# A transformer block in Strassen form: another order of the MLP's buffers, the last sum of y behind attention's sums, and an operand's sums later

## The chip, the cores and the metric

The kernel runs on one core of one Trainium2 chip. The metric is the time of one execution on the device, in microseconds. The kernel before took 735.64 us, the median of 3 runs (734.81 to 736.56).

## What is computed

One cross-attention block with its MLP, all in float32. `x` and `ctx_2048` are both 8 x 256 x 512. The block's batch is 8, its queries come from `x`, its keys and values from `ctx_2048`; there are 16 heads of 32.

```python
x = layer_norm(hidden_states, ln1_w, ln1_b)
q = (x @ q_w + q_b)                      # 512 -> 512, then 16 heads of 32
k = (encoder_hidden_states @ k_w + k_b)
v = (encoder_hidden_states @ v_w + v_b)
attn = softmax(mask(q @ k.T / sqrt(32)))
out = (attn @ v) @ cproj_w + cproj_b
hidden = out + residual                  # residual: hidden_states
y = layer_norm(hidden, ln2_w, ln2_b)
y = gelu(y @ fc_w + fc_b)                # 512 -> 2048, tanh form
return hidden + y @ proj_w + proj_b      # 2048 -> 512
```

## The kernel before

**Groups and stages.** The 8 batch rows are taken two at a time: four groups, g = 0 to 3, of 512 tokens. A first stage makes attention for all four groups; a second stage, the MLP, then runs over the four groups again. Between the stages the hidden state of each group lies in DRAM (`hid_dram`), and `load_hid` brings it back.

**Strassen products.** Each large matrix product is a 2 x 2 block product in Winograd's form of Strassen: seven block products in place of eight, and sums of blocks before and after. An operand is a tile of seven slots: the quarters 11, 12, 21, 22 and three sums. `A_SUMS` are the four sums of a weight operand, `B_SUMS` those of a token operand (the last is t4 = 21 - t2, written after attention's tokens have been turned into columns). `sum_up` makes them one by one. The first MLP product (512 -> 2048) uses the form twice, one inside the other: seven outer products, k = 0 to 6 (`product`), each of seven inner ones (`sub`). So its weight is seven operands of seven slots, each 1792 KB. They are made once, during attention, kept in `w2_dram`, and loaded again for each group by `load_w2`, into four places that are reused in turn. Each call of `product` ends with the load into the place that it has just read; SP issues that load when the product's last matmul is done.

**Attention's order.** The work is written out by hand. A unit is a pair of batch row and 128 columns of heads (8 units in a group). For a unit the kernel turns the probabilities of unit n (`turn_probs`), divides those of unit n + 1 on POOL (`divide`), makes the scores of unit n + 2, and calls what is listed for places in the unit: `between[g, u, i]` holds pieces with matmuls (the projections of the next group, the output projections of earlier ones), `aside[g, u, i]` holds sums, loads and stores; aside 0 runs ahead of the division, 1 to 3 behind it, in this order. `begin` and `spread` fill these lists. `split("b", (i, g, u, at), ...)` lists sum i of the weight operand b (outer operand s3) at such places, all on POOL. Each engine, and SP's queue of DMA issues, works in the order in which the calls are made.

**The end of attention.** After the last unit comes the output projection of group 3 (`project_out(3)`, tiles po). Its second inner product reads the sums of the attention tile, which `sum_att(3, NHG - 1, V)` makes on DVE (tile as, line 735). Group 0's y, the MLP's first input, has its four sums on DVE listed in units 6 and 7 of group 3 (line 993; tile y, line 219), and `split_y` makes the sums of the inner form between the pieces of po (line 307). `project_out` adds the bank to a tile of the residual (resx, 2 KiB per partition, one for each quarter: res11, res12, res21, res22) on POOL (line 630) and stores it to `hid_dram` (line 631).

**The MLP.** In an outer product, the first bank is copied to u1 (ACT, line 1276), u2 = bank 6 + u1 and u3 = bank 7 + u2 follow on DVE (line 1121, a helper that records all such adds). Bank 7 is then accumulated further by TensorE, after u3 has read it. The results go to the hidden quarters h11, h12, h21, h22 or, through a working tile s3 (`hs` in the trace), by POOL adds to several of them. Product 0 writes h21 alone, product 1 h11, product 3 h12, product 4 h22. Between the products the gelus of finished quarters run on ACT. Then seven products with the second weight follow (tiles pw, banks py). The residual comes back into resm (`residual`, line 290) and receives the result.

**Buffers.** A pool gives its tiles addresses in the order of their first call. The MLP's pools lie over those of attention; a tile waits for whatever last used its memory, a DMA's read of it included. In KiB of a partition, near the top:

| attention | at | MLP before | at |
|---|---|---|---|
| pr (probabilities, 3) | 176.4 to 200.4 | h21 | 181.9 to 189.9 |
| v (2) | 200.4 to 204.4 | h22 | 189.9 to 197.9 |
| pt (turned probabilities, 4) | 204.4 to 212.4 | s3 | 197.9 to 205.9 |
| res11 | 212.4 to 214.4 | u1 | 205.9 to 207.9 |
| res12 | 214.4 to 216.4 | u2 (2) | 207.9 to 211.9 |
| res21 | 216.4 to 218.4 | u3 | 211.9 to 213.9 |
| res22 | 218.4 to 220.4 | resm | 213.9 to 221.9 |

Of the kernel before, what the change touches and what calls it, by code (L numbers as in the profile page):

```python
# [10 lines left out]
F32 = mybir.dt.float32  # L11
# [5 lines left out]
P = 128  # L17
# [5 lines left out]
def tile_xattn_block(  # L23
# [62 lines left out]
    HI, HC, HF, HD2 = INNER // 2, NC // 2, NF // 2, D // 2  # L86
# [57 lines left out]
    def place(name, at):  # L144

        return Operand(wts.tile([P, 7, HC, S], F32, tag=f"w{at}", name=name))
# [23 lines left out]
    def rows_of(t):  # L170
        return t.rearrange("p i h s -> p i (h s)")
# [16 lines left out]
    def load_w2(at):  # L188
# [20 lines left out]
    B_SUMS = (  # L209
        ("t1", "12", "11", ALU.subtract),  # L210
        ("t2", "22", "t1", ALU.subtract),
        ("12", "22", "12", ALU.subtract),
        ("t4", "21", "t2", ALU.subtract),
    )

    def sum_up(eng, x, table, *which):
        for i in which:
            to, a, b, op = table[i]
            eng.tensor_tensor(x[to], x[a], x[b], op)
# [73 lines left out]
    ys, hids, y2s = {}, {}, {}  # L293
# [29 lines left out]
    with ExitStack() as att:  # L323
        work = att.enter_context(tc.tile_pool(name="attwork", bufs=2))
# [289 lines left out]
        def load_res(g, *which):  # L614
            for n in which:
                r = work.tile([P, 2, S], F32, tag=f"res{n}", bufs=1, name=f"resx_{g}_{n}")
                nc.sync.dma_start(r, quarter_of(group_of(xf, g), n))
                res[g, n] = r
# [108 lines left out]
        def sum_att(g, hg, eng=nc.gpsimd):  # L727

            x, h = att_in[g], hg % HC
            for to, a, b in (  # L730
                (("t1", "12", "11"),)
                if hg < HC
                else (("t2", "22", "t1"), ("12", "22", "12"), ("t4", "21", "t2"))
            ):
                eng.tensor_tensor(x[to][:, h, :], x[a][:, h, :], x[b][:, h, :], ALU.subtract)
# [10 lines left out]
        def begin(g, u, i, f, *args):  # L746
            aside[g, u, i].append(lambda: f(*args))

        def spread(g, places, pieces):

            for i, f in enumerate(pieces):
                begin(g, *places[min(i, len(places) - 1)], f)
# [31 lines left out]
        V, GP = nc.vector, nc.gpsimd  # L784
# [6 lines left out]
        ALL = (0, 1, 2, 3)  # L791
# [129 lines left out]
        def split(key, *places):  # L921

            for i, *at in places:
                begin(*at, lambda i=i: sum_up(GP, fc[key], A_SUMS, i))
# [3 lines left out]
        sums("b", "a", "b", ALU.subtract, (0, 2, 1), (0, 2, 1), (0, 2, 2), (0, 2, 2))  # L928
        split("a", (0, 0, 3, 1), (1, 0, 3, 2), (2, 0, 3, 2), (3, 0, 4, 1))
        begin(0, 4, 2, keep_own, "a", "11")  # L930
        split("b", (0, 0, 4, 2), (1, 0, 5, 1), (3, 0, 5, 2))
        begin(0, 4, 3, fc_load, "a", "22")

        sums("a", "a", "b", ALU.subtract, (0, 6, 2), (0, 6, 2), (0, 6, 1), (0, 7, 1))
# [25 lines left out]
        g = 1  # L960
        begin(g, 6, 1, load_res, 0, *QUARTERS)
        begin(g, 7, 1, bias_res, 0)
        g = 2
# [6 lines left out]
        g = NG - 1  # L970
# [19 lines left out]
        for c, (u, i) in enumerate(((5, 1), (5, 1), (6, 1), (6, 1))):  # L990
            between[g, u, i].append(lambda c=c: th(c))

        spread(g, [(6, 2), (7, 1), (7, 2), (7, 2)], [lambda i=i: sum_up(V, ys[0], B_SUMS, i) for i in ALL])

        def run(pieces):
            for p in pieces:
# [89 lines left out]
        o = project_out(3)  # L1086
        load_res(3, "12")
        sum_att(3, NHG - 1, V)
        y2 = rows_of(place("y2_0", "v").t).rearrange("p i s -> p (i s)")[:, : 21 * P]
        y2 = y2.rearrange("p (t n s) -> p t n s", t=3, n=7)  # L1090
        for i in ALL:
# [8 lines left out]
    with ExitStack() as mlp:  # L1100
        wpool = mlp.enter_context(tc.tile_pool(name="mlpw", bufs=1, reuse_waits="tile"))
        work = mlp.enter_context(tc.tile_pool(name="mlpwork", bufs=1, reuse_waits="tile"))
# [7 lines left out]
        V, GP = nc.vector, nc.gpsimd  # L1110
# [6 lines left out]
        def mm(ps, lhsT, rhs, first, last):  # L1117
            nc.tensor.matmul(ps, lhsT, rhs, start=first, stop=last, skip_group_check=True)  # L1118

        def add(eng, to, a, b, op=ALU.add):  # L1120
            eng.tensor_tensor(to, a, b, op)  # L1121
# [4 lines left out]
        def load_pw(*which):  # L1126
            for n in which:
                f, d = (int(n[0]) - 1) * HF, (int(n[1]) - 1) * HD2
                nc.sync.dma_start(
                    pw[n], proj_w.rearrange("(c p) n -> p c n", p=P)[:, f : f + HF, d : d + HD2]  # L1130
                )
# [23 lines left out]
        for g in range(NG):  # L1155

            h = {
                n: work.tile([P, 2, HF, P], F32, tag=f"h{n}", name=f"h{n}_{g}")
                for n in ("11", "12", "21", "22", "s3")
            }  # L1160

            def out_quarter(b, k):
# [3 lines left out]
            def us(n, name):  # L1166
                return work.tile([P, 2, S], F32, tag=f"u{n}", bufs=2 if n == 2 else 1, name=f"{name}_{g}")

            def bank_of(n, name):
                return ps_f.tile(  # L1170
                    [P, 2, S], F32, tag=f"f{n}", bufs=2 if n in (1, 5) else 1, name=f"{name}_{g}"
                )
# [18 lines left out]
            def norm_piece():  # L1191

                if g + 1 < NG:
                    if not norm:
                        norm.append(layer_norm(hids[g + 1], f"m{g + 1}", nc.scalar))
                        seen, roots, _ = norm[0]
                        norm.extend([*seen, *roots])
                    norm.pop(1)()
# [14 lines left out]
            def some_gelus(n=3):  # L1213
                for f in gelus[:n]:
                    f()
                del gelus[:n]
# [13 lines left out]
            def block(n, cd):  # L1230
                c, d = int(cd[0]) - 1, int(cd[1]) - 1
                return h[n][:, d, c * HF // 2 : (c + 1) * HF // 2, :]

            def product(k, *sums):


                wt, yn = w2[g, k], QI[FC_ORDER[k][1]]
                bank = {}

                def y_of(n):  # L1240
                    if n in QUARTERS:
                        return ys[g].t[:, yn, int(n[0]) - 1, ts(int(n[1]) - 1, P)]
                    return y2s[g][:, ("t1", "t2", "t4").index(n), yn, :]

                def sub(n, w, b, first, last):
                    if first:
                        bank[n] = bank_of(n, f"pf{n}_{k}").rearrange("p i (j s) -> p (i j) s", j=2)
                    for m in range(HF // 2):
                        mm(
                            bank[n][:, m, :],  # L1250
                            wt[:, QI[w], ts(m, P)],
                            y_of(b),
                            first and m == 0,
                            last,
                        )

                def u(n):
                    return us(n, f"u{n}_{k}").rearrange("p i (j s) -> p (i j) s", j=2)

                def made(cd, n, x):  # L1260
                    some_gelus()
                    if k in (3, 4) and cd != "22":
                        norm_piece()
                    if sums[0][1] is None:
                        add(V, block(sums[0][0], cd), bank[n], x)
                        return

                    r = h["s3"][:, parts[0] % 4 // 2, parts[0] % 2 * HF // 2 :][:, : HF // 2]
                    parts[0] += 1
                    add(V, r, bank[n], x)  # L1270
                    for to, base in sums:
                        add(GP, block(to, cd), block(base, cd), r)

                sub(1, "11", "11", True, False)
                u1 = u(1)
                nc.scalar.copy(u1, bank[1])  # L1276
                sub(6, "s2", "t2", True, True)
                u2 = u(2)
                add(V, u2, bank[6], u1)
                some_gelus()  # L1280
                sub(7, "s3", "12", True, False)
                u3 = u(3)
                add(V, u3, bank[7], u2)
                some_gelus()
                sub(5, "21", "t1", True, False)
                made("22", 5, u3)
                sub(1, "12", "21", False, True)
                some_gelus()
                for to, base in sums:
                    if base:  # L1290
                        add(V, block(to, "11"), bank[1], block(base, "11"))
                    else:
                        nc.scalar.copy(block(to, "11"), bank[1])
                sub(7, "22", "t4", False, True)
                made("21", 7, u2)
                sub(5, "s4", "22", False, True)
                made("12", 5, u2)
                load_w2(w2_place[g, k])
# [8 lines left out]
            product(3, ("12", "21"))  # L1307
            if g == 0:
                load_pw("11", "12", "22")
            product(4, ("22", "12"), ("21", "21"))  # L1310
            if g == 0:
                load_pw("21")
# [139 lines left out]
```

## Time and profile before

| | |
|---|---|
| median of 3 runs | 735.64 us (734.81 to 736.56) |
| the profiled execution | 735.38 us |
| its span | 733.5 us |
| granted TensorE clock, mean over the span | 0.995 |
| TensorE (PE) busy | 722.2 us, 98% of the span |
| POOL, DVE, ACT busy | 502.4, 415.4, 322.3 us |
| moved by DMA | 138.83 MB, mean 189 GB/s |

The profile is of one execution. PE is TensorE's matmuls, PEld its weight loads, DVE VectorE, ACT ScalarE, POOL GpSimd, SP the engine that issues the DMAs here; L1121 is line 1121 of the kernel. A float32 matmul stands twice in the counts: 28 matmuls of an outer product are 56 records. In the strips of slices the span is cut into 40 equal parts of 18.3 us; a digit is the busy share in tenths, and PEclk the granted clock in tenths of full speed. The waits name an engine and line, what ended the wait, the total, the number and the longest. The chain is followed back from the last instruction to what released each step.

### The profile page before, as it was taken

Reading aid. Unit: us, or ns where it says so; the run is one execution under the profiler, and the core shown is the slowest. Engines: PE = TensorE matmul, PEld = TensorE weight load, DVE = VectorE, ACT = ScalarE, POOL = GpSimd, SP = SyncE. Lnnn points to the kernel's source line nnn. Section 1 sums busy time; section 2 is a strip of 40 time slices with the busy share of each in tenths; the row PEclk is TensorE's granted clock in tenths of the full one; section 3 lists DMA queues with packets and bytes.
Section 4 is the critical chain, followed back from the end, with each engine's and each line's share of the span. In section 5 each row is a group of like instructions: output and inputs, shape, how many; then the busy total and the mean of one; then the engine's idle time right before and its main releaser. Section 6 shows DMA issues by size and latency. Waiting matters only on the chain.

```text
span 733.5 us, 14067 instructions
## 1 busy us (share of the span) xinstructions
PE 722.2 (98%) x5109; PEld 630.2 (86%) x5109; DVE 415.4 (57%) x1056; ACT 322.3 (44%) x904; POOL 502.4 (68%) x451
## 2 busy tenths in 40 slices
PE   9999999999999999999799999999999999999998
PEld 7888777887778777778699889998899988999986
DVE  4576756675456566878378585780156811566211
ACT  2277798777676788761034400225002160030500
POOL 3857798987797999886269960589404896048870
PEclk9999999999999999999899999999999999999999
DMA  9516555697639777832699802992019930172001
GB/s 304 186 60 200 207 190 200 200 321 259 221 129 310 251 259 256 295 98 87 229 382 347 347 1 70 390 322 96 0 58 352 338 130 0 58 265 95 1 0 58
DMA packets 75380, 138.83 MB, mean 189 GB/s; under 512 B 6916, under 2 KB 45104, under 8 KB 72624
## 3 DMA queue, kind: packets, MB, share of 16 engines
q1 hardware_dynamic: 75056, 137.91, 53.8%
q8 instruction: 41, 0.67, 0.4%
q14 instruction: 27, 0.22, 0.1%
q0 software_dynamic: 256, 0.02, 0.0%
HBM read 104.36 MB, written 33.55 MB: 188 GB/s over the span
## 4 chain that ended last, share of the span: by engine, by line
PE 91%; POOL 3%; issue 2%; DMA 2%; ACT 2%; DVE 0%; SPq 0%; POOLq 0%; DVEq 0%
PE py L1118 25%; PE pf L1118 23%; PE ppt L699 8%; PE pv L441 7%; PE pqT L441 7%; PE pkT L441 5%; PE s L646 5%; PE av L715 4%; PE po L441 4%; PE pkT L538 2%; POOL resx L630 1%; ACT h L1220 1%; DMA hid_dram<-resx 1%; PE pxt L274 1%; PE pyt L274 1%
## 5 line engine op out<-in xcount | busy, mean ns | idle before, releaser
L1121 POOL TENSOR_TENSOR h<-h,hs 128x512 f32<-128x512 f32 x100 | 126.8, 1291 | 127.0 <-DVE hs L1121 126.4
L1118 PE MATMUL pf<-y,w 128*128 128x128 f32 x1568 | 177.9, 277 | 5.3 <-DVE u L1121 5.3
L1118 PEld LDWEIGHTS pf<-y,w 128*128 128x128 f32 x1568 | 177.7, 194 | 5.7 <-DVE u L1121 5.5
L688 POOL TENSOR_TENSOR pr<-pr,rsum 128x512 f32<-128x512 f32 x128 | 129.5, 1041 | 36.8 <-DVE rsum L686 23.9
L674 ACT ACTIVATE pr<-pr,nmax 128x256 f32<-128x256 f32 x256 | 127.9, 504 | 35.4 <-DVE nmax L664 35.2
L664 DVE CUSTOM_DVE_ANT_0 pr<-s,mb 128x256 f32<-128x256 f32 x256 | 93.6, 414 | 39.2 <-PE s L646 29.1
L1276 ACT COPY u<-pf 128x512 f32<-128x512 f32 x28 | 16.4, 587 | 207.4 <-PE pf L1118 207.4
L1118 PE MATMUL py<-pw,h 128*128 128x256 f32 x384 | 84.9, 379 | 0.0
L1118 PE MATMUL py<-pw_t,h 128*128 128x256 f32 x384 | 84.2, 379 | 0.0
L1118 PEld LDWEIGHTS py<-pw_t,h 128*128 128x128 f32 x384 | 72.7, 190 | 9.8
L1118 PEld LDWEIGHTS py<-pw,h 128*128 128x128 f32 x384 | 72.4, 190 | 9.6
L699 PEld LDWEIGHTS ppt<-ident,pr 128*128 128x128 f32 x512 | 57.3, 140 | 14.9 <-issue 5.9
L699 PE MATMUL ppt<-ident,pr 128*128 128x128 f32 x512 | 68.8, 276 | 0.3
L1121 DVE TENSOR_TENSOR resm<-py,resm 128x512 f32<-128x512 f32 (+1 forms) x21 | 13.6, 664 | 93.6 <-PE py L1118 93.6
L1121 DVE TENSOR_TENSOR u<-pf,u 128x512 f32<-128x512 f32 x56 | 38.7, 691 | 35.2 <-PE pf L1118 24.8
L1121 DVE TENSOR_TENSOR hs<-pf,u 128x512 f32<-128x512 f32 x72 | 49.5, 688 | 13.7 <-PE pf L1118 13.1
L1220 ACT ACTIVATE h<-h,cols 128x256 f32<-128x256 f32 x128 | 52.1, 497 | 10.6 <-POOL h L1121 10.5
L704 ACT COPY pt<-ppt 128x512 f32<-128x512 f32 x96 | 51.9, 575 | 7.0 <-PE ppt L699 7.0
L441 PE MATMUL pv<-vw,ctxT 128*128 128x256 f32 x224 | 52.4, 380 | 0.0
L441 PE MATMUL pqT<-xnT,qw 128*128 128x256 f32 x224 | 51.0, 379 | 0.0
L674 ACT ACTIVATION_READ_ACCUMULATOR pr<-pr,nmax 128x1 f32 x256 | 49.1, 192 | 0.0
L441 PEld LDWEIGHTS pqT<-xnT,qw 128*128 128x128 f32 x224 | 41.4, 190 | 5.0
(145 smaller groups left out, 1041.4 us busy)
## 6 DMA issues: line engine op xcount, KB each, us to landing
w<-w_dram SPq DMA_DIRECT2D x16, 1792.0 KB, 8.4
w<-in_L_xattn_fc_w_dram SPq DMA_DIRECT2D x36, 256.0 KB, 5.6
w<-w_dram SPq DMA_DIRECT2D x12, 768.0 KB, 7.4
ctx<-in_ctx_dram SPq DMA_DIRECT2D x16, 256.0 KB, 4.9
x<-in_x_dram SPq DMA_DIRECT2D x16, 256.0 KB, 4.2
v_dram<-st_v SPq DMA_DIRECT2D x16, 256.0 KB, 2.2
v<-v_dram SPq DMA_DIRECT2D x16, 256.0 KB, 4.4
resx<-in_x_dram SPq DMA_DIRECT2D x16, 256.0 KB, 4.0
```

Of the source, the lines that this page charges most:

```text
L441: nc.tensor.matmul(bank[n][:, i, :], l[:, c, ts(i, P)], r[:, c, :], start=first and i == 0 and c == 0, stop=last and c == HC - 1, skip_gro ...
L646: nc.tensor.matmul(banks[j][:, i, :], qT[j * HD : (j + 1) * HD, b * S + i * P : b * S + (i + 1) * P], kT[j * HD : (j + 1) * HD, b * SK : ( ...
L664: nc.vector.tensor_tensor_reduce(pr[:, j, i, :], banks[j][:, i, :], mbias[g][1][:, b, :], scale=-SCALE, scalar=FLT_MAX, op0=ALU.add, op1=A ...
L674: nc.scalar.activation(pr[:, j, i, :], pr[:, j, i, :], AF.Exp, bias=nmax[:, j, i : i + 1], scale=-1.0, accum_out=sums[:, j, i : i + 1],)
L688: nc.gpsimd.tensor_tensor(pr[:, j], pr[:, j], rsum[:, j, :, None].to_broadcast([P, NQ, SK]), ALU.mult,)
L699: nc.tensor.transpose(ps[:, kc, ts(i, P)], probs[n][:, j, i, ts(kc, P)], ident)
L704: nc.scalar.copy(pt, ps)
L715: nc.tensor.matmul(av[j * HD : (j + 1) * HD, :], vs[g, hg][:, b * NK + kc, ts(j, HD)], pts[n, j][:, kc, :], start=(kc == 0), stop=(kc == N ...
L1118: nc.tensor.matmul(ps, lhsT, rhs, start=first, stop=last, skip_group_check=True)
L1121: eng.tensor_tensor(to, a, b, op)
L1220: nc.scalar.activation(h[n][:, :, p, :], h[n][:, :, p, :], AF.Gelu_apprx_tanh, bias=col(c_fcb, half * HF + p), scale=1.0,)
L1276: nc.scalar.copy(u1, bank[1])
```

## The change

Three edits.

The hidden quarter h22 gets its buffer in product 4's place, after resm, and no longer with the others at the head of a group. So s3, the u's and resm each lie 8 KiB lower, and h22 lies last:

| MLP after | at | over attention's |
|---|---|---|
| s3 | 189.9 to 197.9 | pr |
| u1, u2 (2), u3 | 197.9 to 205.9 | pr, v, pt |
| resm | 205.9 to 213.9 | pt, res11 |
| h22 | 213.9 to 221.9 | res11, res12, res21, res22 |

The fourth sum of group 0's y is called after the last sums of attention, not ahead of them. On DVE it now stands between as (line 735) and the first add of po (line 460).

Three of the four sums of operand b in group 0 are listed later: sum 0 from unit 4 (aside 2) to unit 5 (aside 1), sum 1 from aside 1 to aside 2 of unit 5, sum 3 from unit 5 (aside 2) to unit 6 (aside 0). On POOL this moves one instruction: sum 0 now follows the four instructions of a division that it stood ahead of. The order of all other instructions on all engines, and of the DMA issues, is the same.

```diff
-        split("b", (0, 0, 4, 2), (1, 0, 5, 1), (3, 0, 5, 2))
+        split("b", (0, 0, 5, 1), (1, 0, 5, 2), (3, 0, 6, 0))
...
-        spread(g, [(6, 2), (7, 1), (7, 2), (7, 2)], [lambda i=i: sum_up(V, ys[0], B_SUMS, i) for i in ALL])
+        spread(g, [(6, 2), (7, 1), (7, 2)], [lambda i=i: sum_up(V, ys[0], B_SUMS, i) for i in ALL[:3]])
...
         sum_att(3, NHG - 1, V)
+        sum_up(V, ys[0], B_SUMS, 3)
...
             h = {
                 n: work.tile([P, 2, HF, P], F32, tag=f"h{n}", name=f"h{n}_{g}")
-                for n in ("11", "12", "21", "22", "s3")
+                for n in ("11", "12", "21", "s3")
             }
...
+            h["22"] = work.tile([P, 2, HF, P], F32, tag="h22", name=f"h22_{g}")
             product(4, ("22", "12"), ("21", "21"))
```

## The prediction

> **What bounds the kernel now.** I read the page first: busy shares and the strip of slices, for the engine that fills the span and the slices where it does not.
>
> ```profile
> span 733.5 us, 14067 instructions
> PE 722.2 (98%) x5109; PEld 630.2 (86%) x5109; DVE 415.4 (57%) x1056; ACT 322.3 (44%) x904; POOL 502.4 (68%) x451
> PE   9999999999999999999799999999999999999998
> PEclk9999999999999999999899999999999999999999
> ```
>
> TensorE is busy in 98% of the span, so only time in which TensorE stands still or runs slowly can be won. One slice shows both, the 20th (348.4 to 366.8 us): busy 7, clock 8. That is where attention gives way to the MLP. Next, the waits between 345 and 365 us (engine and line, releaser: total, times, longest):
>
> ```profile
> DVE u L1121 <- DMA hid_dram<-resx: 6.5, 1, 6.5
> PE pf L1118 <- DVE u L1121: 5.3, 1, 5.3
> ```
>
> Then the chain that ended last, in order of time (start, length, what), across that place:
>
> ```profile
> 346.34 1.17 POOL resx L630
> ...
> 347.56 1.25 POOL resx L630
> 348.82 8.41 DMA hid_dram<-resx
> ...
> 357.41 0.70 DVE u L1121
> ...
> 358.16 35.22 PE pf L1118 x296
> ```
>
> A DVE add in the MLP's first product waits for a store of attention's residual, and TensorE waits for the add. The add does not use that data. In the built program u3 of product 0 lies at 211.9 to 213.9 KiB of each partition, and the residual tile res11, being stored, at 212.4 to 214.4: the wait is for the memory. The stretches around it show the clock (length; busy PE, PEld, DVE, ACT, POOL; granted clock, DMA share, GB/s):
>
> ```profile
> 354.00:356.00 2.00, 0.00 (x0) 0.00 (x0) 0.00 (x0) 0.00 (x0) 0.00 (x0) 0.83 0.81 293
> 356.00:358.00 2.00, 0.00 (x0) 0.00 (x0) 0.59 (x1) 0.00 (x0) 0.00 (x0) 0.50 1.04 366
> 358.00:360.00 2.00, 1.84 (x8) 1.85 (x9) 0.79 (x2) 0.00 (x0) 0.00 (x0) 0.50 0.09 30
> 360.00:362.00 2.00, 2.00 (x12) 2.00 (x11) 0.72 (x2) 0.00 (x0) 0.00 (x0) 0.50 0.00 0
> 362.00:364.00 2.00, 2.00 (x19) 2.00 (x19) 0.68 (x2) 0.59 (x1) 0.00 (x0) 0.96 0.64 115
> ```
>
> The gap is paid twice: while TensorE waits, and again at half clock until about 362. Last, the issues of SP, because each weight load there waits for the last matmul of a product:
>
> ```profile
> 348.39 0.34 SPq L200 DMA_DIRECT2D w<-w_dram  x1
> 348.82 3.42 SPq L631 DMA_DIRECT2D hid_dram<-resx  x4
> 361.97 0.33 SPq L200 DMA_DIRECT2D w<-w_dram  x1
> ...
> 368.38 0.32 SPq L200 DMA_DIRECT2D w<-w_dram  x1
> ...
> 374.63 0.32 SPq L200 DMA_DIRECT2D w<-w_dram  x1
> ```
>
> **The buffers.** With h22 placed last, s3 and the u's each lie 8 KiB lower, and resm too. u1 to u3 now lie at 197.9 to 205.9 KiB, over probabilities, v and pt. In the built program u3 of product 0 no longer waits for a store; u1 waits for a POOL division and u2 and u3 for the two last loads of v, issued by 317.73 with 4.4 us to landing at the median, some 30 us before use.
>
> What product 0 costs now: its first matmul starts at 348.19, the load behind it is issued at 361.97, 13.78 us. In the next group the same stage starts at 450.28 and that load goes out at 456.56, 6.28 us. Difference 7.50 us. It is made of 5.33 of waiting, 1.95 of half clock (the last two of seven sub-products take 358.16 to 361.90 = 3.74 us, where two sevenths of 6.25 are 1.79), and 0.22 of edges. Product 1 takes 368.38 - 361.97 = 6.41, product 2 374.63 - 368.38 = 6.25: another 0.16. **Gain 7.66 us**, if nothing else is late.
>
> On the clock the page "TensorE: Matmul & The Clock Gate" of the Trainium skill (Part 1: The HAM clock gate) says that about 3.4 us without work halves the clock and about 3.4 us of work restores it. By it the half clock would cost 1.7 us, and the gain would be 5.33 + 1.7 = 7.0; the trace has about 3.9 us of work at clock 0.50, and its 7.66 is what I use.
>
> What is late next? First u3 itself: in product 1 TensorE starts at 361.9 and the pair of u2 and u3 is done at 365.50, 3.6 us in, while sub-product six begins 4.5 us in: 0.9 us spare. Then the weights. The load for product 2, issued at 348.39 with 8.2 us to landing, is there at 356.6; product 2 would start at 348.19 + 2 x 6.25 = 360.7: 4.1 spare. The loads for products 3 to 6 are issued behind products 0 to 3, so they move with TensorE; before, they land 3.9, 3.3, 2.4 and 2.2 us ahead of need (issue plus landing of 8.7, 9.2, 9.9 and, for the last piece, 7.4 us, against product starts 374.6, 380.9, 387.0, 393.2).
>
> One thing doesn't move with them: the residual's stores and the load for product 2, 2.88 MB, are queued at 348.4 to 352. By 354 the rows (108, 244, 401 GB/s in three stretches of 2 us) have moved 1.51 MB; 1.38 MB remain, at 0.40 MB/us until 357.4. The load for product 3, issued at 348.19 + 6.28 = 354.5, would by itself flow from 355.9 (the old one, issued at 361.97, moved a third of the full rate over 362 to 364, so it flowed from some 1.4 us after issue); so it lags 1.5 us. That is under all four, 2.2 to 3.9, and the stretch 382 to 388 has DMA shares of only 0.82, 0.82 and 0.75, where it is worked off. I cost it at 0; if the remainder leaves at the 293 GB/s of 354 to 356, until 358.7, the lag is 2.8 and product 5 or 6 waits some 0.6 us.
>
> "DMA: Bandwidth & Descriptors" (Queues, rings and completion order) says that on each DMA engine descriptors are consumed in ring order: the rule that speaks against this change, since it makes the load stand behind the stores. Without it the lag would be 0, with it the 1.5 above; TensorE's time is the same by both.
>
> The residual's stores still end at 357.2. Their new successors are h22, first written in product 4 (before at 385.7, now some 378), and resm's load (368.8, now some 361): both later. But h22's first POOL, DVE and ACT instructions carry 4, 5 and 7 waits more. The chain shows satisfied steps of 0.03 to 0.05 us at DVE (357.23 to 357.41). POOL has 1.69 us idle there, DVE is busy 5.33 of 6.25; ACT's 7 x 0.05 = 0.35 stand in the gelus of 397 to 406.7, ahead of a place where TensorE waits 0.3 for POOL. Between 0 and 0.35 I take **+0.2**.
>
> **The last sum of y.** Attention's three DVE sums (0.41 each) now start one y sum earlier, at about 336.6 instead of 337.69. TensorE waits for the first: ten matmuls of 0.216 from 335.58 end at 337.74, the next starts at 338.16, 0.42 lost. The y sum goes behind them, ahead of u1, whose read must precede the next accumulation. The two y sums took 1.2 each beside POOL's adds; POOL is idle from 337.22 to 342.66, so it should not be slower than 1.2 there. At best all 0.42 is won; at worst the sum takes 1.64, as one did at 332.76, and u1 and TensorE come 0.44 late. I take **-0.35**, near the better end.
>
> **The sums of operand b.** The first of four POOL sums (1.27 us, at 101.89) moves behind a division that starts at 103.17 and can't start before its reciprocal ends at 103.03: 0.14 earlier. Its result is transposed at 110.55, 3.3 us after it ends. The other two move without changing POOL's order. Behind them POOL idles 2.40 us before 112.19 and takes the 1.27. Nothing of SP's queue moves, and the chain from 84 to 130 us is TensorE alone. Cost 0, bounds -0.14 and +0.14.
>
> **Sum**, against this execution's 735.38 us (span 733.5 and 1.88 around it): -7.66 + 0.2 - 0.35 = -7.81, 727.57. The median of the three runs, 735.64, lies 0.26 higher: **727.8 us**.
>
> **Rivals.**
> *The transfers eat part of it.* The lag above is larger and products 3 to 6 or the projection weights wait (the third of these is issued at 387.2 with 12.8 us to landing, 400.0, and DVE uses it from 400.82). For: DMA shares near 1 from 364 to 418. Against: spare of 2.2 to 4 us, and TensorE waited for no load there. Price 1 to 3 us: 729 to 731.
>
> *No effect.* Another tile under u1 to u3 holds the same store, or the wait only moves to h22 or resm. For it speaks that the stores still land at 357.2; against it the addresses. 735.4.
>
> *Slower.* The load for product 3 comes so late that TensorE idles at about 366.7 and drops to half clock again. The slowest load of weights in this stretch took 17.4 us (issued at 404.7 into a full queue): 354.5 + 17.4 = 371.9, 5.0 of waiting plus the 2.1 (1.95 and 0.16) of half clock, 7.1 lost of the 7.8 gained, 735. It decides from about 18.1 us of landing on; at 19, with 8.7 lost, 736.5. Against it: 8.7 us at this issue now.
>
> **How the numbers follow.** The forecast has 0.80, transfers 0.14, no effect 0.04, slower 0.02. A time is told from no change at about 0.2% (1.5 us): faster 0.94, same 0.04, slower 0.02. The lower end takes the sum's best terms (no extra waits, 0.42, 0.14: 727.2) and the spread of runs (0.8): 726.4. The upper takes in the transfers up to 2.4 us: 730.2.
>
> **What would show it.** Right: no gap of PE between 345 and 365 us, clock 1.00 throughout, product 0 in 6.3 us, no chain step through hid_dram<-resx, PE's wait for as gone. Wrong: a wait of pf for w (transfers), for u again (no effect), or a second dip of the clock near 367 (slower).

## The result, and the profile after

| | before | after |
|---|---|---|
| median | 735.97 us (734.81 to 736.56, 4 runs) | 728.04 us (727.24 to 729.32, 4 runs) |
| the profiled execution | 735.38 us | 727.24 us |
| its span | 733.5 us | 725.1 us |
| granted TensorE clock | 0.995 | 1.000 |

After over before is 0.9896, 95% interval 0.9876 to 0.9916: about 1% faster, 6.2 to 9.1 us. The forecast was 727.8, with a range of 726.4 to 730.2.

The page of the kernel after, its span, TensorE's share and the two strips of slices:

```profile
span 725.1 us, 14073 instructions
...
PE 719.1 (99%) x5109; PEld 627.6 (87%) x5109; DVE 416.9 (57%) x1056; ACT 321.8 (44%) x904; POOL 501.8 (69%) x451
...
PE   9999999999999999999999999999999999999998
...
PEclk9999999999999999999999999999999999999999
```

The 7 and the 8 of the 20th slice are gone. The chain that ended last (start, length, what) across the place where the store stood:

```profile
335.41 1.19 DVE as L735
...
338.53 8.90 PE po L441 x40
347.43 37.53 PE pf L1119 x336
```

No step goes through `hid_dram<-resx` any more: from 338.53 the chain is TensorE alone for 46 us (line 1119 is the former 1118). In its place a short piece of DVE has come up, which is taken up below. SP's issues, each weight load behind the last matmul of a product:

```profile
347.46 0.34 SPq L200 DMA_DIRECT2D w<-w_dram  x1
347.89 3.42 SPq L631 DMA_DIRECT2D hid_dram<-resx  x4
353.71 0.33 SPq L200 DMA_DIRECT2D w<-w_dram  x1
...
359.96 0.32 SPq L200 DMA_DIRECT2D w<-w_dram  x1
...
366.22 0.32 SPq L200 DMA_DIRECT2D w<-w_dram  x1
```

Products 1 and 2 follow at 6.25 us. The stores are issued as late as before against TensorE's work; nothing waits for them.

**Step by step.** TensorE has the same 5109 matmul records in the same order in every kernel here, so they can be compared one by one. The table gives how much later (+) or earlier (-) a record starts than in the profiled execution of before, in us, at six of its times: two before the change reaches the critical place, the start of po of group 3, the start of product 0, after product 0, and near the end.

| kernel | 112 | 296 | 334.7 | 348.2 | 363.5 | 720 |
|---|---|---|---|---|---|---|
| all three edits (after) | -0.88 | -0.88 | -0.89 | -0.93 | -8.41 | -8.40 |
| e1 buffers alone | -0.74 | -0.74 | -0.75 | -0.75 | -8.24 | -8.24 |
| e2 y sum alone | -0.35 | +1.06 | +1.06 | +1.01 | +1.93 | +1.92 |
| e3 b sums alone | -0.88 | -0.87 | -0.88 | -0.91 | -0.83 | -0.84 |
| e4 store first | -0.75 | -0.09 | -0.10 | -0.12 | -7.61 | -7.61 |
| e5 4 adds | -0.74 | -0.15 | -0.16 | -0.20 | -4.41 | -4.41 |
| e6 10 adds | -0.86 | -0.86 | -0.86 | -0.91 | +1.15 | +1.15 |
| e7 y behind u1 | -0.55 | -0.55 | -0.56 | -0.51 | -8.00 | -7.99 |
| e8 y behind u2 | +0.70 | +0.70 | +0.70 | +0.42 | -7.06 | -7.06 |
| e9 first norm later | -0.32 | -0.32 | -0.32 | -0.60 | -8.08 | -8.09 |

Differences along a row are what counts. The first column differs from execution to execution whatever the kernel. Two things make it in the first 8 us: TensorE waits at about 6 us for the first weights of K (0.4 us in before, 1.5 in e8), and its clock comes up early or late (in after matmuls speed up at 4.7 us, from starts 0.21 us apart to 0.11; in before at 7.2 us). In the row of after, all of the gain is between 348.2 and 363.5, which is product 0 and the first 1.5 us of product 1: **8.41 - 0.93 = 7.48 us**. After it nothing is won or lost.

### The profile page after: what moved, and what is told of

Its sections match the earlier page's. It is cut to its first block, busy times and chain, and to the rows that moved or that the text cites. A ratio compares the mean times of both kernels' runs of the same rounds, so it can differ in the third digit from the quotient of the medians.

```text
span 725.1 us, 14073 instructions
## 1 busy us (share of the span) xinstructions
PE 719.1 (99%) x5109; PEld 627.6 (87%) x5109; DVE 416.9 (57%) x1056; ACT 321.8 (44%) x904; POOL 501.8 (69%) x451
## 4 chain that ended last, share of the span: by engine, by line
PE 95%; ACT 1%; issue 1%; POOL 1%; DVE 1%; DMA 1%; SPq 0%; ACTq 0%; DVEq 0%; POOLq 0%
PE py L1119 25%; PE pf L1119 23%; PE ppt L699 8%; PE pv L441 7%; PE pqT L441 7%; PE po L441 6%; PE pkT L441 5%; PE s L646 5%; PE av L715 4%; PE pkT L538 2%; PE pxt L274 1%; PE pyt L274 1%; ACT h L1221 1%; PE pct L274 1%; DMA kw<-in_L_xattn_k_w_dram 1%
## 5 line engine op out<-in xcount | busy, mean ns | idle before, releaser
L1119 PEld LDWEIGHTS pf<-y,w 128*128 128x128 f32 x1568 | 175.7, 192 | 0.2
L1119 PE MATMUL pf<-y,w 128*128 128x128 f32 x1568 | 175.7, 275 | 0.0
```

## Experiments: which edit it was

My theory: the whole gain is that u3 of product 0 no longer lies over res11. The rival: the sums carry a part.

**e1, the buffers alone.**

```diff
-                for n in ("11", "12", "21", "22", "s3")
+                for n in ("11", "12", "21", "s3")
...
+            h["22"] = work.tile([P, 2, HF, P], F32, tag="h22", name=f"h22_{g}")
             product(4, ("22", "12"), ("21", "21"))
```

> Only the order of the buffers is changed; both orders of the sums stay as before. Memory theory (all of the gain is u3 of product 0 no longer lying over res11): product 0 of the first MLP group takes 6.45 us instead of 13.78, TensorE is 7.5 us earlier from there to the end, 728.4. Rival, the sums carry a part of the gain (I forecast 0.35 us for the last sum of y): 0.3 to 0.4 us less than with all three edits, that is, TensorE starts product 0 with the 0.42 us loss of before still in the step ahead of it and nothing made up.

Measured: 728.12 us, ratio 0.9901 (0.9885 to 0.9917). Product 0 gains 8.24 - 0.75 = 7.49 us, against 7.48 with all three edits. The buffers carry all of it. TensorE's wait for attention's first sum stays (PEld 0.6, PE 0.2 us).

**e2, the last sum of y alone.**

```diff
-        spread(g, [(6, 2), (7, 1), (7, 2), (7, 2)], [lambda i=i: sum_up(V, ys[0], B_SUMS, i) for i in ALL])
+        spread(g, [(6, 2), (7, 1), (7, 2)], [lambda i=i: sum_up(V, ys[0], B_SUMS, i) for i in ALL[:3]])
...
         sum_att(3, NHG - 1, V)
+        sum_up(V, ys[0], B_SUMS, 3)
```

> Only the last sum of y moves behind attention's. Memory theory: the gap at the first of attention's sums (0.42 us) goes and the store still ends the wait of u3; what is won ahead of it is lost in it, 735.6 to 736, product 0 still 13 to 14 us with a dip of the clock. Rival (this edit is worth its 0.35 us by itself): the stores also come 0.35 earlier and the end moves by that.

Measured: 735.89 us, ratio 1.0001 (0.9986 to 1.0015). The waits of this kernel from 333 to 366 us:

```profile
DVE u L1122 <- DMA hid_dram<-resx: 6.3, 1, 6.3
...
PE pf L1119 <- DVE u L1122: 5.2, 1, 5.2
...
PEld po L441 <- DVE po_u L460: 0.5, 1, 0.5
```

The stall is the one of before. In po the wait for as is replaced by one for u1, and TensorE gains 0.05 us (+1.06 to +1.01). Product 0 took 0.92 us longer than in before although the wait was no longer (5.2 against 5.33); the clock was at half for longer, as shown below.

**e3, the sums of operand b alone.**

```diff
-        split("b", (0, 0, 4, 2), (1, 0, 5, 1), (3, 0, 5, 2))
+        split("b", (0, 0, 5, 1), (1, 0, 5, 2), (3, 0, 6, 0))
```

> Only the three sums of operand b in group 0 are listed later. Memory theory: no step of TensorE moves by more than 0.1 us, 735.6 to 736. Rival (the division of unit 6 is held up and TensorE with it): TensorE earlier by up to 0.14 us from 110 us on.

Measured: 735.32 us, ratio 1.0000 (0.9990 to 1.0011). TensorE's records keep their distance over the place (-0.87 at 105, -0.88 at 112 and 292). This edit does nothing to the time. Product 0 takes 0.07 us longer than in before, by another split that is taken up below.

## Experiments: is it the store?

**e4, the old buffers, with the store of res11 ahead of the weight load.** If the wait for the store is the cause, the store can be made early instead of moving what waits for it.

```diff
-        load_w2("c")
-        run(later)
+        run(later[:1])
+        load_w2("c")
+        run(later[1:])
```

> The buffers and sums of before; only the store of res11 is issued ahead of the weight load of product 2 instead of behind it, so u3 still waits for that store. Memory theory: the wait was long because the store stood behind a load of 1792 KB and TensorE's last matmul of attention; issued at about 344.8 with 2.3 to 4 us to landing it is done by 349, u3 (351) no longer waits, product 0 takes 6.45 us, TensorE is 7.4 to 7.5 us earlier to the end, 728.4. Rival (the old place of the u's is slow for another reason, or any store near there holds product 0): product 0 stays at 10 to 14 us, 732 to 736.

Measured: 728.14 us, ratio 0.9904 (0.9885 to 0.9923). Product 0 gains 7.61 - 0.12 = 7.49 us. SP's issues in this kernel:

```profile
344.61 0.37 SPq L631 DMA_DIRECT2D hid_dram<-resx  x1
348.27 0.34 SPq L200 DMA_DIRECT2D w<-w_dram  x1
```

The store goes out 3.7 us ahead of the load, lands 3.5 us later, at 348.1, and u3 over the same old memory is not held. So the addresses matter only through this one wait. In before POOL had finished res11 at 344.70, but SP, which issues in order, sent the store at 348.82, behind the load that waits for po's last matmul. It then took 8.41 us beside that load (DMA share 0.65 to 1.11 over 348 to 354); sent ahead of the load, with little else moving (share 0.17 over 346 to 348), it took 3.5.

## Experiments: what a stall costs

The chip's clock took a part of the loss. To measure it without a wait for a DMA, TensorE is stalled at the same place of the changed kernel by extra DVE adds ahead of u3; their result is overwritten. e5 has 4 of them, e6 has 10:

```diff
+                for _ in range(4 if g == 0 and k == 0 else 0):
+                    add(V, u3, u2, u2)
                 add(V, u3, bank[7], u2)
```

> The changed kernel with 4 more DVE adds (u3 = u2 + u2, overwritten by the right u3) ahead of u3 in product 0 of the first group: a short wait of TensorE put back at the same place. Each add 0.6 to 0.7 us, u3 was 0.9 us early, so TensorE waits 1.6 to 1.9 us. Gate theory (the clock halves only after more than about 2.4 us without work): product 0 grows by the wait alone, 1.6 to 1.9 us, clock 1.00. Rival (every wait costs 1.4 times its length, as 7.5 for 5.33): 2.2 to 2.7 us.

> The same with 10 more adds: TensorE waits 5.1 to 6.0 us with no DMA in the way. Gate theory: the wait and then 3.5 to 4 us at clock 0.50, so product 0 and 1 together grow by the wait plus 1.8 to 2.2 us, 7 to 8 us: the loss of before comes back whole, without any overlap of buffers. Rival (the half clock came from the transfers, not from TensorE's idleness): the wait alone, 5.1 to 6.0 us.

Both adds-to-wait estimates were too small: the adds took 1.0 and 0.84 us each, not 0.6 to 0.7, so TensorE waited 3.0 and 7.4 us. Both theories are read against the waits as measured. TensorE's wait in e5:

```profile
PE pf L1119 <- DVE u L1122: 3.0, 1, 3.0
```

and the stretches of e5 around it (length; busy PE, PEld, DVE, ACT, POOL; granted clock, DMA share, GB/s):

```profile
352.00:354.00 2.00, 0.62 (x6) 0.43 (x4) 1.93 (x3) 0.59 (x1) 0.78 (x1) 1.00 1.09 337
354.00:356.00 2.00, 0.37 (x3) 0.37 (x4) 1.76 (x4) 0.00 (x0) 0.00 (x0) 1.00 0.79 280
```

The wait in e6:

```profile
PE pf L1119 <- DVE u L1122: 7.4, 1, 7.4
```

and the stretches of e6:

```profile
356.00:358.00 2.00, 0.00 (x0) 0.00 (x0) 1.90 (x4) 0.00 (x0) 0.00 (x0) 0.62 0.65 229
358.00:360.00 2.00, 0.72 (x3) 0.72 (x4) 1.79 (x3) 0.00 (x0) 0.00 (x0) 0.50 0.00 0
360.00:362.00 2.00, 2.00 (x11) 2.00 (x10) 0.63 (x2) 0.00 (x0) 0.00 (x0) 0.50 0.00 0
362.00:364.00 2.00, 2.00 (x14) 2.00 (x14) 0.78 (x2) 0.00 (x0) 0.00 (x0) 0.67 0.00 0
```

In e5 the clock stays at 1.00. Product 0 is 3.27 us longer than in after (7.48 - 4.21): the wait of 3.01, and 0.26 more for stopping and starting again, called edges below. In e6 the clock falls, and the product is 9.54 longer (7.48 + 2.06): 7.37 of waiting, 0.26 of edges taken over from e5, and the remaining 1.91 of half clock. A loss of 1.4 times each wait would have been 4.2 and 10.3; it is refuted by e5. Before splits in the same way: 7.48 = 5.33 + 0.26 + 1.89.

That the transfers lower the clock is refuted too. In e5 it stays at 1.00 beside them, and so it does in after, where TensorE does not stop:

```profile
356.00:358.00 2.00, 2.00 (x21) 2.00 (x20) 1.65 (x3) 0.00 (x0) 0.00 (x0) 1.00 1.19 414
```

In e6 it stays at 0.50 while the DMA engines are idle (share 0.00 from 358).

The recorded gate theory has one figure that fails: a fall after more than about 2.4 us without work. In e5 TensorE stood still for 3.0 us and the clock did not fall; in e3 it fell 2.0 us after the last matmul, which ended at 351.92. The wait of e3, and two stretches:

```profile
PE pf L1118 <- DVE u L1121: 5.9, 1, 5.9
```

```profile
352.00:354.00 2.00, 0.00 (x0) 0.00 (x0) 0.00 (x0) 0.58 (x1) 0.00 (x0) 0.97 1.02 315
360.00:362.00 2.00, 2.00 (x17) 2.00 (x17) 1.36 (x2) 0.00 (x0) 0.00 (x0) 0.82 0.00 0
```

The clock of 0.97 and of 0.82, a mean of full and half, puts the fall at 353.9 and the return at 360.7. What the four falls have in common stands in the clock records of the traces: in before, e2, e3 and e6 alike the clock is at 0.50 for 6.83 us, wherever in this time TensorE resumes. The stretches at 1.00 ahead of the falls (348.16 or 351.57 us) and behind them (372.05) are 102, 103 and 109 times half of this, 3.41 us. So in these traces the clock changes in fixed steps, and the loss is set by how much of the 6.83 us is left when work resumes: 2.9 us in e3, 4.0 in before and e6, 6.2 in e2. By the split above it costs 1.34 (7.55 - 5.95 - 0.26), 1.89 and 1.91, and 2.94 us (8.40 - 5.20 - 0.26). Where a wait falls within the steps no edit here controls.

## Experiments: the piece of DVE that came up

In the kernel after, DVE adds of po stand behind work for y, and TensorE waits for them. Its DVE timeline there (start, length, operation, tiles):

```profile
334.48 0.71 DVE L219 TENSOR_TENSOR y<-y 128x512 f32<-128x512 f32 x1
335.41 1.19 DVE L735 TENSOR_TENSOR as<-att,as 128x256 f32<-128x256 f32 x1 [0.22 <-ACT att L723]
336.52 0.41 DVE L735 TENSOR_TENSOR att<-att 128x256 f32<-128x256 f32 x1
336.86 0.41 DVE L735 TENSOR_TENSOR as<-att,as 128x256 f32<-128x256 f32 x1
337.19 0.68 DVE L219 TENSOR_TENSOR y<-y 128x512 f32<-128x512 f32 x1
337.80 0.68 DVE L460 TENSOR_TENSOR po_u<-po,cb 128x512 f32<-128x512 f32 x1
```

The first sum of attention takes 1.19 us, not 0.41: it starts beside POOL's residual adds (332.92 to 336.32) and ends only after them. u1 (po_u) comes at 337.80 and TensorE's next matmul at 338.53, behind it.

**e7, the last sum of y behind u1.**

```diff
         sum_att(3, NHG - 1, V)
-        sum_up(V, ys[0], B_SUMS, 3)
...
             run(o[i : i + 1])
+            if i == 0:
+                sum_up(V, ys[0], B_SUMS, 3)
             split_y(0, y2, i)
```

> The changed kernel, with the last sum of y one place further back on DVE, behind u1 of po (line 460). In the changed kernel TensorE's wait for attention's sum has gone to u1: PEld waits 0.5 us for it. Theory: u1 starts 0.6 us earlier, that wait goes, and TensorE is 0.4 us earlier from there to the end, 727.6. Rival (what is late next takes it, split_y or u2): 0 to 0.1 us.

Measured: 727.21 us, ratio 0.9892 (0.9875 to 0.9908). The rival holds: TensorE is 0.42 us earlier at 339.8 (-0.56 to -0.98) and has lost it at 343.1 (-0.55). Its waits there:

```profile
PE po L441 <- DVE po_u L465: 0.2, 1, 0.2
```

Line 465 is u2: DVE still had the sum and a split of y, 1.7 us, ahead of it.

**e8, all of this y work one piece further back.**

```diff
-        for i in ALL:
-            run(o[i : i + 1])
-            split_y(0, y2, i)
-        run(o[4:])
+        run(o[:2])
+        sum_up(V, ys[0], B_SUMS, 3)
+        for i in ALL:
+            split_y(0, y2, i)
+            run(o[i + 2 : i + 3])
+        run(o[6:])
```

> The changed kernel, with the last sum of y and the four splits of y each one piece of po further back on DVE: u1 and u2 of po now come directly behind attention's sums. In the trace of the run before this one the 0.42 us won at u1 were lost again at u2 (DVE has 1.7 us of y work ahead of it). Theory (TensorE waits for whichever of DVE's adds stands behind the y work): u2 is done by about 339 and TensorE, which needs its bank at about 340.4, no longer waits: 0.4 us earlier from there to the end, 727.6. Rival (the work only has to be done somewhere in these 12 us and takes the time at the next add, made or u3): 0 to 0.1 us.

Measured: 727.92 us (727.29 to 730.72, 4 runs), ratio 0.9898 (0.9871 to 0.9925). TensorE keeps 0.42 us as far as 343.1 (+0.70 to +0.28), gives 0.14 back by 348.2, and has 0.28 in the end, against 0.04 in the kernel after. The median can't show a quarter of a microsecond; the records do. Both theories are half right: most of the wait goes, and one third of it comes up again at a later add (st_o, line 629).

**e9, the first statistics one place later as well.**

```diff
-            g, hids, 0, "m", [(1, 1), (1, 2), (2, 1), (2, 2), (2, 2), (3, 1), (3, 2), (4, 1), (4, 2)], V
+            g, hids, 0, "m", [(1, 2), (1, 2), (2, 1), (2, 2), (2, 2), (3, 1), (3, 2), (4, 1), (4, 2)], V
```

> The kernel of the run before this one, and the first statistics of group 0's hidden state one place later in unit 1 of group 3. In the profiles so far DVE waited 0.8 to 2.5 us there for the load of hm, and TensorE lost 0 to 1.4 us in the step behind it (0 where DVE waited up to 1.1). Theory: DVE's wait goes, no TensorE step near 293 us is lost in any execution, and the times spread less: 727.0 to 727.4. Rival (the load is as late for the new place, or the two statistics together hold DVE up): 0 to 1.4 us lost there as before.

Measured: 727.44 us (727.19 to 727.57, 4 runs), ratio 0.9884 (0.9869 to 0.9898). This is for the runs that differ at 293 us, where the first statistics of hm wait for its load. Here is that wait in after, which lost nothing there, and in e2, which lost 1.41 us (-0.35 to +1.06):

```profile
DVE st_m L244 <- DMA hm<-hid_dram: 1.1, 1, 1.1
```

```profile
DVE st_m L244 <- DMA hm<-hid_dram: 2.5, 1, 2.5
...
PE s L646 <- DVE nmax L664: 0.7, 1, 0.7
```

In e4 and e5 DVE waited 1.8 and 1.7 us and TensorE lost 0.67 and 0.59; elsewhere DVE waited 0.7 to 1.1 and TensorE nothing. In e9 DVE has no such wait. Its four runs lie within 0.4 us, those of after within 2.1; but those of e7, with the old place, lie within 0.7, so that the times spread less is not shown. That e9 is faster than the change is shown for 0.24 us by the records of po, in one execution of each; by their medians the two can't be told apart.

## Why the prediction was right

The time and the cause were right, with two terms mis-sized and one that was not needed. That the forecast lies within 0.3 us of the median is in part luck: -0.35 and +0.2 were both wrong and partly cancel. And the stall itself cost 7.48 us in the one execution that was read, but 7.55 in e3 and 8.40 in e2.

- **The stall of product 0**: forecast 7.66, measured 7.48 (7.49 in e1 and e4). The 0.17 lie in "the same stage starts at 450.28": that is where the chain's piece begins; the first matmul of that stage starts at 450.11, so an undisturbed product 0 up to the next load takes 6.45 us, which is what after shows (347.26 to 353.71), not 6.28. The 0.16 at the start of product 1 were right.
- **The half clock**: 1.95 in product 0 and 0.16 in product 1 forecast, with 0.22 of edges; by the split above 1.89 and 0.26 in all. The prediction read it from its trace; the figure of 1.95 is no constant (1.34 to 2.94 above).
- **The last sum of y**: forecast -0.35, measured -0.04, between the ends given (+0.44 to -0.42) but far from the value taken. The step that failed is "Attention's three DVE sums (0.41 each) now start one y sum earlier". They did start earlier, but the first took 1.19 where it took 0.41 in before, since it now stood beside POOL's adds. The slow place stayed and another instruction stood in it: the 1.2 of "The two y sums took 1.2 each" is the mean of one at 0.73 and this fourth one at 1.75, which took 0.68 in its new place. So u1 starts at 337.80 against 338.70 in before, no earlier once the 0.89 us of the row are taken off, and the wait for as became one for u1. The prediction's own prices give no more: three sums from 336.6 and then 1.2 put u1 at about 338.7. The dependence of the accumulation on u1's read was in the prediction, but only for its worse end.
- **The sums of operand b**: 0 forecast, 0 measured (e3).
- **The 16 waits of h22's first instructions**: +0.2 taken, 0 measured: the row of after stays within 0.01 us of -8.41 from 363.5 to 409. What they cost their own engines was not followed.
- **What is late next, the weights**: right. The lag of the load for product 3 was forecast as 1.5 us. It was issued at 353.71 with 9.9 us to landing (8.7 before), 363.6, and product 3 starts at 374.6 - 8.4 = 366.2, 2.6 ahead instead of 3.9. The next two land 10.6 and 11.4 us after their issues (9.2 and 9.9), so product 5 has 1.0 us left of 2.4; by product 6 the lag is worked off (2.6 ahead). Measured lag 1.3 to 1.5 us. TensorE waits for none of them, so the rival of the transfers fell, with 1 us to spare.
- **The sum**: -7.81 forecast; the records give 7.48 + 0.04 = 7.52; the difference of medians, 7.93, holds both in its interval. The spans of the two profiled executions differ by 8.40, and 0.88 of this is there at 112 us, from the first weights (0.42) and the clock's first rise; it is no part of the change.

On the clock, "TensorE: Matmul & The Clock Gate" of the Trainium skill (Part 1: The HAM clock gate) puts both ways at about 3.4 us and says that the window runs freely. The runs agree with the second more than with the first: the changes lie whole multiples of 3.41 us apart, but the clock fell 2.0 us after the last matmul in e3, 2.5 in before and 4.6 in e6 and e2, and not within the 3.0 us of e5. It came back 2.9 us after work began in e3, 4.0 in before and e6 and 6.2 in e2, which is why about the same wait cost e2 0.92 us more.

## What to carry to other kernels

When an engine waits for a transfer of data that it doesn't use, look at the addresses: a buffer may lie over one whose store is still queued. It can be mended from either side, by giving that memory to the tile needed last, or by issuing the store ahead of the large load in the same queue; both gave the same 7.49 us here. Price a stall of TensorE as its length and a range for the half clock, not one figure: nothing for the 3.0 us of e5, 1.3 to 2.9 us for waits of 5.2 to 7.4 us here. On an in-order engine that is full, moving one instruction ahead of another can move the wait to the one that was overtaken, as it did in after, so read which adds the next consumers need before counting a gain.

## What I had not expected

- A DVE add of two SBUF operands of 128x256 took 1.19 us where it began beside a POOL add, and ended 0.3 us after it; alone it took 0.41.
- The profiled executions differ by up to one or two microseconds at two places that have nothing to do with the change: the start, with the first weights of K and the clock's first rise (TensorE between 0.70 later and 0.88 earlier than in before), and the load of hm at 293 us (0 to 1.41 us). A difference of two single profiles holds both; record by record they drop out.
- One wait for memory cost 1% of a kernel in which TensorE was busy for 98% of the span.
